# A graph-attention stack: when a one-head layer's row of G goes to memory and back

## The chip, the cores and the metric

The kernel runs on one core of a Trainium2 chip. The metric is the device time of one execution in microseconds (us). The core has five engines that run side by side: TensorE (PE in the profile, with its weight loads as PEld), VectorE (DVE), ScalarE (ACT), GpSimd (POOL) and SyncE (SP). SP issues nearly all DMA transfers of this kernel.

## The reference, cut to what matters

There are 16 graphs of 1024 nodes with 256 features, one adjacency matrix for all, and four layers. Each layer adds a graph-attention block to x:

```python
h = jnp.maximum(_layernorm(x), 0.0)
x = x + GNN(h, adj, W, a)
# in each GNN, with H heads (4, 1, 4, 1) of D = 256 / H features:
Wh = h @ W
e = leaky_relu(e_src[:, None] + e_dst[None, :])   # e_src, e_dst: Wh times the two halves of a
e = where(adj, e, -inf)
out = elu(softmax(e, axis=-1) @ Wh)               # relu in the last layer
```

Layers 0 and 2 have four heads, layers 1 and 3 have one. They differ in the slope of the leaky relu and in how adj becomes a mask.

## The kernel before, in words

**Softmax in factors.** exp(leaky_relu(s + d)) is a maximum of two products. The kernel therefore needs no exponential per pair of nodes. It has, for every node as a neighbour, a column factor `rcol` and a scale that is multiplied into `whx` (the projected features with a column of ones for the row sums), and for every node as a receiver a factor `gcol`. A tile of weights is `w = max(g, rcol) * mask`, where `g` is gcol laid out as a row and repeated on all 128 partitions. One DVE instruction makes 128 neighbours by 1024 receivers (`weights`, L455). TensorE then multiplies such tiles with `whx` and accumulates in PSUM (`aggregate`, L472), and ACT copies the sums out (L487).

**How G becomes a row.** `gcol` is spread over partitions. `rows` (L397 to L406) turns it on TensorE (L402), copies the result from PSUM to the tile `gT` on ACT (L404), and has SP write it to a buffer in device memory, `grow` (L406). `fetch` (L425 to L431) reads `grow` back repeated on all partitions, into `gs` (512 KB, L430). The fetch must wait until the write has landed. `broadcast` (L433 to L441) copies `gs` into the PSUM tile `g` on ACT (L441). For a four-head layer `gT` has 32 rows and there are four fetches; for a one-head layer it has 8 rows and there is one.

**How a layer's input is prepared.** `preparation(n)` lists 21 pieces: statistics of the two halves of x; normalise half 0 and half 1 (L334); then for each half a transposition, and eight projections of 128 nodes (`project`, L376 on TensorE, L378 on ACT); then `factors` (gcol, L394 and L395), `rows`, `fetch_heads`, and an empty piece. In nearly all layers the transposition is done by a DMA: `split` has ACT separate the 16-bit halves of the words (L343) and SP issue a transposing transfer (L345); `merge` has ACT put the halves together again (L351), which waits for that transfer. Each preparation has two such transfers, one a half.

**Order of the work.** Each graph is a stream of four layers; four streams are in flight and `order_of_steps` interleaves them, so that from step 7 on nearly all steps alternate between a four-head and a one-head layer of different graphs. A step is eight groups of matmuls. For a one-head layer a group is 128 receivers; for a four-head layer it is half the receivers of one head. Every engine gets its instructions in the order in which the program emits them, and works through them in that order; waits on semaphores do the rest.

Preparation runs ahead: step n is prepared while steps n - 2 and n - 1 aggregate. A table of due times, one number a piece, says behind which group each piece is emitted: `start = 8 * (n - 2)`, and `ONE`, `FOUR`, `NEXT`, `TIGHT` and others are the tables (L51 to L59). `ONE` is used by most one-head layers. Pieces fall due by time, and at the same time in the order of the steps (the sort at L611). A due time of 8 or more lies in the step just before, so 11 is behind group 3 of the four-head step n - 1.

Around the change, in a four-head step n - 1, the pieces of two layers meet: the end of the preparation of the one-head layer n (projections 4 to 7 and factors, behind group 0), and the start of the preparation of the four-head layer n + 1 (normalise and split of half 0 behind group 0, of half 1 behind group 1, merge of half 0 behind group 3, merge of half 1 behind group 4, its first four projections behind group 5). Fetches are limited by `fetch_heads`, which keeps at most two heads ahead of the G that has been copied, and `gs` has two buffers. PSUM has four banks for sums, projections and the transposed gcol, which are taken in turn (`bank`).

Of the kernel before, what the change touches and what calls it, by code (L numbers as in the profile page):

```python
# [50 lines left out]
FOUR = (-8, -8, -5, 0, 1, 0, 3, 5, 5, 5, 5, 1, 4, 5, 5, 5, 5, 6, 8, 8, 10)  # L51
SHORT = (-4, -4, -4, 0, 1, 0, 3, 5, 5, 5, 5, 1, 4, 5, 5, 5, 5, 6, 8, 8, 10)
NEXT = (-4, -4, -4, 1, 3, 2, 5, 8, 8, 8, 8, 4, 7, 8, 8, 8, 8, 9, 10, 10, 12)
ONE = (2, 2, 2, 3, 4, 3, 5, 7, 7, 7, 7, 4, 7, 8, 8, 8, 8, 8, 11, 11, 12)
SOON = (0, 0, 0, 1, 2, 1, 3, 4, 4, 5, 5, 2, 5, 6, 6, 7, 7, 7, 8, 8, 10)
FIRST = (-4, -4, -4, -2, -0.9, -1, -1, -0.8, -0.8, -0.8, -0.8, 0, 0, 1, 1, 1, 1, 1, 2, 2, 4)
TIGHT = (4, 4, 4, 5, 6, 5, 7, 8, 8, 8, 8, 6, 8, 9, 9, 9, 9, 9, 10, 10, 12)
# [13 lines left out]
def kernel(ctx: ExitStack, tc: tile.TileContext, x, adj, ws, avs, out):  # L71
# [417 lines left out]
    def slack(n):  # L489

        return LAYERS[steps[n + 1][1]][0] == 1
# [153 lines left out]
    for n, (b, l) in enumerate(steps):  # L645
# [6 lines left out]
        start = 8 * (n - 2)  # L652
        kind = ONE if LAYERS[l][0] == 1 else SOON if n < 3 else FOUR
        if kind is FOUR and free > start + kind[0]:
            kind = SHORT if slack(n - 2) else NEXT
        if kind is ONE and free > start + kind[0]:
            kind = TIGHT
# [120 lines left out]
```

## Time and profile before

| | us |
|---|---|
| median of 3 runs | 2448.24 |
| lowest, highest | 2442.77, 2450.0 |
| the profiled execution | 2449.74 |
| its span, first to last instruction | 2448.0 |

| engine | busy us | share of the span |
|---|---|---|
| PE (matmul) | 2394.8 | 98% |
| PEld (weight load) | 2153.2 | 88% |
| DVE | 2040.0 | 83% |
| ACT | 1480.0 | 60% |
| POOL | 1073.7 | 44% |

The granted clock of TensorE was 0.997 of full speed. All numbers of the profile are from one execution. Busy time is time in which an engine has an instruction under way; for TensorE, whose matmuls overlap, the gaps say more than the busy share. A wait is written as "engine, tile, line <- what released it", with the total, the count and the longest. The chain is found by going back from the last instruction to what released each. "SPq" is SP's queue of DMA instructions; a DMA's landing is a time of its own, later than its issue.

### The profile page before, as it was taken

To read this page: it belongs to the slowest core of one execution; us is meant where nothing else is said; L and a number is where in the kernel's file an instruction comes from. 1 tells how busy PE (TensorE), PEld (TensorE's weight loads), DVE (VectorE), ACT (ScalarE), POOL (GpSimd) and SP (SyncE) were. 2 spreads that over 40 slices of the span, in tenths; PEclk is the share of its full clock that TensorE was granted. 3 is DMA by queue.
4 is the path that set the end of the run, shared out by engine and by line. 5 is a ranking of instruction groups with operands and counts; after the bars stand their busy time and mean duration, and the time that the engine had idled before them with its cause. 6 is when DMAs were issued, how large, how long until landed. Compare 5 with 4: busy or idle time off the path is not lost.

```text
span 2448.0 us, 86681 instructions
## 1 busy us (share of the span) xinstructions
PE 2394.8 (98%) x39177; PEld 2153.2 (88%) x39177; DVE 2040.0 (83%) x2141; ACT 1480.0 (60%) x2505; POOL 1073.7 (44%) x1350
## 2 busy tenths in 40 slices
PE   7999999999999999999999999999999999999999
PEld 5888899899888888898998888888988998988987
DVE  8988588898888988887988888888889888888794
ACT  5465676565666656765656765566655577656542
POOL 3345455433345454544433554543443345545331
PEclk9999999999999999999999999999999999999999
DMA  5322233243333222323433322224334323223220
GB/s 182 83 53 63 45 79 67 66 114 92 85 96 79 72 63 52 74 71 96 114 89 88 80 62 71 64 50 108 75 93 114 95 48 80 68 65 76 75 54 35
DMA packets 292220, 191.84 MB, mean 78 GB/s; under 512 B 261778, under 2 KB 264586, under 8 KB 289930
## 3 DMA queue, kind: packets, MB, share of 16 engines
q1 hardware_dynamic: 291840, 186.29, 30.6%
q8 instruction: 307, 5.03, 0.9%
q14 instruction: 63, 0.52, 0.1%
q10 hardware_dynamic: 10, 0.00, 0.0%
HBM read 104.87 MB, written 17.43 MB: 50 GB/s over the span
## 4 chain that ended last, share of the span: by engine, by line
PE 82%; ACT 7%; DMA 5%; DVE 4%; issue 2%; POOL 0%; SPq 0%; DVEq 0%; ACTq 0%
PE bank L472 64%; PE bank L376 17%; DVE w L455 2%; DMA gs<-grow 2%; ACT rows L334 2%; DMA grow<-gT 2%; ACT g L441 1%; ACT rows L343 1%; ACT rows L525 1%; ACT rows L351 1%; ACT y L487 1%; DVE bn L287 1%; DMA rows<-rows 0%; PE bank L402 0%; ACT whx L378 0%
## 5 line engine op out<-in xcount | busy, mean ns | idle before, releaser
L472 PE MATMUL bank<-whx,w 128*64 128x65 f32 x36864 | 1898.0, 240 | 17.9 <-DVE w L455 9.3
L472 PEld LDWEIGHTS bank<-whx,w 128*64 128x64 f32 x36864 | 1745.7, 144 | 173.9 <-ACT whx L378 21.8
L455 DVE SCALAR_TENSOR_TENSOR w<-g,rcol,mask 128x1024 f32<-128x1024 f32 (+1 forms) x1288 | 1540.2, 1270 | 204.0 <-PE bank L472 165.2
L388 POOL TENSOR_TENSOR whx<-whx 128x1024 f32<-128x1024 f32 x128 | 244.5, 1910 | 819.1 <-ACT whx L386 819.1
L487 ACT ACTIVATE y<-bank 128x260 f32<-128x260 f32 (+1 forms) x504 | 192.1, 381 | 567.7 <-PE bank L472 567.7
L376 PE MATMUL bank<-wx,rows 128*128 128x264 f32 (+1 forms) x2048 | 484.8, 390 | 15.4 <-ACT y L487 11.8
L376 PEld LDWEIGHTS bank<-wx,rows 128*128 128x128 f32 x2048 | 380.9, 190 | 90.9 <-ACT y L487 17.9
L519 POOL TENSOR_TENSOR y<-y,r 128x1024 f32<-128x1024 f32 x124 | 259.0, 2098 | 222.0 <-DVE rows L518 188.4
L334 ACT ACTIVATE rows<-x,shift,rstd 128x256 f32<-128x256 f32 x512 | 265.2, 591 | 66.7 <-POOL shift L328 62.2
L378 ACT ACTIVATE whx<-bank 128x264 f32<-128x264 f32 (+1 forms) x512 | 193.7, 388 | 184.9 <-PE bank L376 184.6
L532 POOL TENSOR_TENSOR x<-x,rows 128x1024 f32<-128x1024 f32 x94 | 222.4, 2365 | 177.9 <-DVE rows L531 177.9
L351 ACT ACTIVATE rows<-rows 128x2048 uint16<-128x2048 uint16 x122 | 261.6, 2144 | 22.7 <-DMA rows<-rows 22.6
L343 ACT ACTIVATE rows<-rows 128x2048 uint16<-128x2048 uint16 x122 | 233.3, 1912 | 3.9
L531 DVE SCALAR_TENSOR_TENSOR rows<-rows,y 128x1024 f32<-128x1024 f32 x94 | 186.6, 1986 | 42.8 <-ACT rows L525 39.1
L287 DVE BATCH_NORM_STATS2 bn<-x 128x6 f32<-128x256 f32 x512 | 175.8, 412 | 34.5 <-POOL x L532 31.1
L441 ACT ACTIVATE g<-gs 128x1024 f32<-128x1024 f32 x158 | 161.8, 1024 | 67.1 <-DMA gs<-grow 55.9
L322 POOL TENSOR_TENSOR rstd<-rstd,neghalf 128x4 f32<-128x4 f32 (+1 forms) x97 | 121.3, 1251 | 41.1 <-DVE shift L323 33.8
L525 ACT ACTIVATE rows<-rows 128x1024 f32<-128x1024 f32 x96 | 100.7, 1048 | 4.2 <-DVE rows L554 4.2
L508 DVE RECIPROCAL r<-y 128x32 f32<-128x32 f32 (+1 forms) x63 | 17.4, 277 | 100.9 <-ACT y L487 100.9
L518 DVE SCALAR_TENSOR_TENSOR rows<-y,r 128x1024 f32<-128x1024 f32 x58 | 70.2, 1251 | 1.1
L386 ACT ACTIVATE whx<-whx,nbias 128x16 f32<-128x16 f32 (+1 forms) x128 | 40.4, 316 | 4.2
L384 ACT ACTIVATE rcol<-whx,rbias 128x16 f32<-128x16 f32 (+1 forms) x128 | 40.0, 313 | 4.2
(82 smaller groups left out, 461.9 us busy)
## 6 DMA issues: line engine op xcount, KB each, us to landing
gs<-grow SPq DMA_DIRECT2D x158, 512.0 KB
x<-in_x SPq DMA_DIRECT2D x15, 1024.0 KB
out<-x SPq DMA_DIRECT2D x30, 512.0 KB
w<-in_adj SPq DMA_DIRECT2D x8, 512.0 KB
rows<-rows SPq DMA_TRANSPOSE x122
x<-in_x SPq DMA_DIRECT2D x2, 512.0 KB
wx<-in_L_gnn_W SPq DMA_DIRECT2D x8, 128.0 KB
out<-x SPq DMA_DIRECT2D x8, 128.0 KB
```

The source lines that it names most:

```text
L287: nc.vector.bn_stats(bn[:, c, :], xs[b][:, c, :])
L334: nc.scalar.activation(xn[:, :, q, :], xs[b][:, c, :].rearrange("p (k i) -> p k i", k=K), AF.Relu, bias=st["shift"][:, c:c + 1], scale=st[ ...
L343: nc.scalar.activation(bits, xn.rearrange("p (n s) -> p s n", s=2), AF.Copy)
L351: nc.scalar.activation(st["hT", half].rearrange("p k i -> p (k i)").bitcast(U16).rearrange("p (n s) -> p n s", s=2), st["turned", half].re ...
L376: nc.tensor.matmul(pw, lhsT=st["hT", half][:, k, q * P:(q + 1) * P], rhs=wx[l][:, k, :], start=(k == 0), stop=(k == K - 1))
L378: nc.scalar.activation(st["whx"][:, c, :], pw, AF.Copy)
L388: nc.gpsimd.tensor_tensor(wh[:, :, :, 0:D], wh[:, :, :, 0:D], wh[:, :, :, D:D + 1].to_broadcast([P, HALF, H, D]), op=ALU.mult)
L455: nc.vector.scalar_tensor_tensor(state[n]["w", h, j][:, s], state[n]["g", h][:, s], state[n]["rcol"][:, j, h:h + 1], masks[LAYERS[steps[n] ...
L472: nc.tensor.matmul(acc[o % P:o % P + cols, q, :], lhsT=st["w", h, jc][:, o:o + cols], rhs=st["whx"][:, jc, h * (D + 1):(h + 1) * (D + 1)], ...
L487: nc.scalar.activation(st["y"][:, i0:i0 + per, h, :], acc, AF.Copy)
L519: nc.gpsimd.tensor_tensor(yh, yh, rb, op=ALU.mult)
L532: nc.gpsimd.tensor_add(xh, xh, e)
```

## The change

One table of due times is edited. In `ONE`, the pieces `rows` and `fetch_heads` (the 19th and 20th numbers) are due at 9 in place of 11. Pieces of the same due time are emitted in the order of the steps, so both come ahead of the normalise and split of half 1 of layer n + 1, which are due at the same time.

```diff
-ONE = (2, 2, 2, 3, 4, 3, 5, 7, 7, 7, 7, 4, 7, 8, 8, 8, 8, 8, 11, 11, 12)
+ONE = (2, 2, 2, 3, 4, 3, 5, 7, 7, 7, 7, 4, 7, 8, 8, 8, 8, 8, 9, 9, 12)
```

## The prediction

> **What bounds the kernel now.** I read the page first (busy shares, then the chain that ended last), next the waits by pair of engines, then the chain and the ACT timeline inside one period.
>
> ```profile
> PE 2394.8 (98%) x39177; PEld 2153.2 (88%) x39177; DVE 2040.0 (83%) x2141; ACT 1480.0 (60%) x2505; POOL 1073.7 (44%) x1350
> ...
> PE 82%; ACT 7%; DMA 5%; DVE 4%; issue 2%; POOL 0%; SPq 0%; DVEq 0%; ACTq 0%
> ```
>
> TensorE sets the time: it is idle for 2448.0 - 2394.8 = 53.2 us, and in the trace some 30 us of that lie in the start and the tail. From 400 to 2330 us its gaps over 0.1 us add up to only 17.8 us. So whatever the change does to DMAs or ACT, it can gain no more than TensorE gaps that it removes. The waits say which those are:
>
> ```profile
> ACT g L441 <- DMA gs<-grow: 55.9, 29, 4.6
> ...
> DVE w L455 <- ACT g L441: 24.5, 14, 11.9
> ...
> PE bank L376 <- ACT y L487: 11.8, 14, 2.0
> ```
>
> The columns are the total in us, the count and the longest. ACT waits 29 times for the fetched row of G (gs); TensorE waits 14 times, 11.8 us in all, at a projection (L376) for ACT's L487. One period of a four-head and a one-head layer shows that these are one thing. Its chain (start, us, what):
>
> ```profile
> 1544.70 1.05 ACT rows L525
> 1545.76 0.27 ACT y L487
> 1546.03 0.15 ACT gT L404
> 1546.17 0.36 SPq L345
> 1546.54 0.05 issue
> 1546.59 3.33 DMA grow<-gT
> 1549.92 0.02 issue
> 1549.94 4.59 DMA gs<-grow
> 1554.53 0.02 issue
> 1554.56 1.03 ACT g L441
> 1555.58 0.31 ACT y L487
> 1555.89 0.04 issue
> 1555.94 4.72 PE bank L376 x20
> ```
>
> and ACT in the same stretch:
>
> ```profile
> 1540.52 2.07 ACT L334 ACTIVATE rows<-x,shift,rstd 128x256 f32<-128x256 f32 x4
> 1542.61 1.91 ACT L343 ACTIVATE rows<-rows 128x2048 uint16<-128x2048 uint16 x1
> ...
> 1549.85 2.16 ACT L351 ACTIVATE rows<-rows 128x2048 uint16<-128x2048 uint16 x1 [0.80 <-DMA rows<-rows]
> 1554.56 1.03 ACT L441 ACTIVATE g<-gs 128x1024 f32<-128x1024 f32 x1 [2.54 <-DMA gs<-grow]
> ```
>
> ACT works in order: second merge (L351, waits for the second transposing transfer), copy of G (L441, waits for gs), then the L487 that frees the PSUM bank which the fourth projection needs. TensorE did three projections (12 matmuls) and then stood 0.44 us, from 1555.50 to 1555.94. Two transfers therefore end ahead of that L487, the fetch of gs and the second transpose, and gs now ends last by 2.54 us.
>
> **What the skill says.** The Trainium skill, DMA: Bandwidth & Descriptors, section "Queues, rings and completion order": SP owns one row of rings, and each DMA engine takes a ring's descriptors in ring order. The trace agrees: the grow write, issued 2.04 us behind the second transpose, landed 0.15 us after it (1549.92 against 1549.77, from the completion events). The same page, "Two DMAs through the same engine are not ordered": a DMA that reads what another wrote needs its completion semaphore. So SP must stand at the gs issue until grow has landed; here it did, from 1547.4 to 1549.94. And "Rules for kernel authors": a transpose beside ordinary DMAs needs no extra care, so nothing but ring order and that SP wait keeps the two apart.
>
> **The change, part by part.** No instruction is added or removed. The built order has four moves in 28 of 31 one-head layers. TensorE's 8-row transpose (L402) goes from behind group 3 to behind group 1 of the four-head layer; ACT's gT copy (L404) goes ahead of the second normalise (L334 x4); SP's grow write and gs fetch go ahead of the second transpose. DVE and POOL are unchanged.
>
> - *TensorE's transpose*: 0.27 us either way. Its operand gcol is ready (ACT L395 ends 1534.53, group 1 ends near 1537) and its bank was freed by a projection's copy. Without that lead it would stand about 1 us a layer; the trace has 2 us of it. Cost 0.
> - *ACT*: the copy starts at 1540.52, 5.4 us sooner than 1545.92. It delays the second normalise and split by 0.15 us (L404 at 1545.92, its follower at 1546.07).
> - *SP and the grow write*: issued at 1540.8, behind the first transpose (issued 1538.47, landed 1544.39). By ring order it lands at 1544.39 + 0.17 = 1544.56. SP issues gs at 1544.6.
> - *The wait added*: the second transpose now queues on SP behind the gs issue, which waits for grow. Its data are ready at 1544.67 (L343's end plus 0.15); SP is free at 1544.6 + 0.4 = 1545.0. It goes out at 1545.0 in place of 1544.55. Over 27 periods worked out alike, this delay is 0.2 us in 15 and at most 1.8. Behind it on SP stand stores and a load of x in some periods, else nothing for over 20 us.
> - *The rings*: gs's 4 KB packets run from 0.6 to about 3.0 us after its issue (1550.5 to 1553 in this period); a transpose's packets begin 1.17 us after its own. The trace of before has no transpose just behind a gs fetch in the steady part, so I bound it. Low end: they share engines freely, 0. High end: the transpose starts when gs's packets end, 1544.6 + 3.0 - (1545.0 + 1.17) = 1.4 us later. One case at the start, a transpose issued 1.67 us after a gs, began 2.6 us after issue instead of 1.17 and landed 7.35 us after it; that speaks for the high end, which I take.
> - *Then ACT*: the second transpose took 5.22 us from issue to landing here (4.2 to 6.3 over the periods, median 5.5). It lands at 1545.0 + 5.22 + 1.4 = 1551.6, where it landed at 1549.77. Merge to 1553.7, G copy without a wait to 1554.7 (gs landed near 1549), L487 ends at 1555.05, 0.84 us sooner than 1555.89. TensorE wanted the bank at 1555.50: the 0.44 us go, with 0.45 to spare.
>
> The same sum for each of the 27 periods from 330 to 2330 us: before, TensorE stands 10.9 us in all (11.8 with the smaller waits that the view counts there); after, 1.3 us, in three periods. With the low end of the rings it is 0. L487 is 3.1 us sooner at best (near 1108) and 1.7 us later at worst (near 581, where TensorE had 1.8 us in hand). So the sum is -9.7 us at the high end of the rings and -10.9 at the low. Landings of the second transpose scatter by 2 us from period to period and will fall differently; I take 1.2 us off for that: **-8.5 us**. On the profiled execution (2449.74 us, span 2448.0) that is 2441.2; on the median of the runs, 2448.24, which is 1.5 us less, 2439.7. I say 2440. The stall that goes leaves TensorE's own work as the next limit; nothing is late behind it, since DVE has its G sooner too.
>
> **Rivals.**
>
> - *The second transpose takes gs's place.* For it: it is the other transfer ahead of the same L487, it is delayed by SP's wait and by gs's packets, and in 14 of the 27 periods TensorE had no gap to give back. Against: gs ends up to 4.6 us behind it now. If it lands 1.2 us later than I worked out in every period, the waits become 11.4 us in place of 10.9: no gain, 2449. At half of that, about -6. This case: 2442 to 2451.
> - *Slower.* The same place, past its break-even of 1.2 us: merge L351 late, L487 late, and TensorE stands at the fourth projection in nearly every period, also where it does not now. At 1.5 us later than worked out the sum is +6.1 us (2454); at 2.0 us it is +19 (2467). The price rises steeply since all 27 periods then pay. It needs a transpose to be slowed by more than ring order: the case at the start of the kernel landed 7.35 us after its issue, and 6.5 is the mean that I already have.
> - *The change doesn't do what it says*: the gs buffer or the limit on fetches ahead could hold the fetch back. The built order has the fetch straight behind the write, and its buffer's last reader, ACT's copy for head 2, ended near 1523. Excluded; what remains would be within 0.3%.
>
> **How the numbers follow.** Case one, -7 to -11 us (2437 to 2441.5): 0.44. The transpose eats the gain: 0.35. Slower: 0.21. A measurement of this kernel tells about 0.3% (7.3 us) from no change, so faster means below 2440.9 and slower above 2455.6. Most of case one is faster (0.40), its rest and case two are the same (0.41), and of case three 0.19 passes the bound. The range runs from 2435 (all 11.8 us gone, and runs as low as before's lowest against its median, leaving out 0.05) to 2457, which leaves out the worse part of the slow case, about 0.13. The likeliest case alone: 2436 to 2443.
>
> **What would show it.** Right: ACT's wait for gs at L441 (55.9 us) falls to a third or less; TensorE's wait at L376 for L487 falls from 11.8 to 1 to 3 us; ACT's wait at the second L351 for its transpose grows from under 1 to about 2 us a period; the grow write lands just after the first transpose. Wrong: a wait at L376 of 10 us or more with ACT's L351 behind a transpose (first rival), TensorE gaps at L376 in over 20 periods (second), or DMA time of the transposes from issue to landing over 8 us. A loss with no more waiting at L376 would mean something that I have not seen: gaps in TensorE's own instruction supply ("issue", 6.7 us at L472 now) while gs and transposes crowd the DMA engines.

## The result, and the profile after

The changed kernel is slower. Its median is 2457.06 us (12 runs, 2454.53 to 2465.24) against 2444.06 us for the kernel before on the same chips (12 runs, 2436.89 to 2454.72). The ratio is 1.0053, 95% interval 1.0036 to 1.0069. The forecast was 2440, in a range of 2435 to 2457.

The profiled execution of the changed kernel took 2462.47 us, with a span of 2460.7, which is 12.7 us more than before. Both profiled executions lie some 5.5 us over the median of their twelve runs, so the two profiles can be held against each other. These are the lines of its page that answer to those of before, busy shares and chain:

```profile
PE 2397.4 (97%) x39177; PEld 2159.4 (88%) x39177; DVE 2039.2 (83%) x2141; ACT 1480.1 (60%) x2505; POOL 1073.3 (44%) x1350
...
PE 92%; DVE 4%; issue 2%; ACT 1%; DMA 0%; DVEq 0%; ACTq 0%
```

The DMAs are gone from the chain that ended last (5% before, 0% now) and ACT is nearly gone (7% before). TensorE is nearly all that is left (92%), and still the kernel is longer. Two waits of the kernel before, to compare with (total us, count, longest):

```profile
ACT rows L351 <- DMA rows<-rows: 22.6, 22, 2.2
...
PE bank L472 <- issue: 6.7, 12, 1.8
```

The waits of the changed kernel:

```profile
ACT rows L351 <- DMA rows<-rows: 61.3, 26, 4.4
PEld bank L472 <- issue: 46.7, 67, 2.4
PE bank L472 <- issue: 31.0, 28, 2.3
...
ACT g L441 <- DMA gs<-grow: 3.1, 3, 1.6
...
PE bank L376 <- ACT y L487: 0.7, 1, 0.7
```

Three of these lines went the way that was forecast. ACT's wait for gs fell from 55.9 us to 3.1, TensorE's wait at the projections from 11.8 to 0.7, and ACT's wait for the transposes grew from 22.6 to 61.3. The new line is TensorE's wait for "issue", that is, for nothing that the profile shows: 6.7 us before, 31.0 now.

The account closes. These are the two groups of TensorE on the page, before and then after (busy us, mean ns, idle time ahead, what ended most of it):

```profile
L472 PE MATMUL bank<-whx,w 128*64 128x65 f32 x36864 | 1898.0, 240 | 17.9 <-DVE w L455 9.3
...
L376 PE MATMUL bank<-wx,rows 128*128 128x264 f32 (+1 forms) x2048 | 484.8, 390 | 15.4 <-ACT y L487 11.8
```

```profile
L472 PE MATMUL bank<-whx,w 128*64 128x65 f32 x36864 | 1901.7, 241 | 41.3 <-issue 31.0
...
L376 PE MATMUL bank<-wx,rows 128*128 128x264 f32 (+1 forms) x2048 | 483.3, 391 | 2.0 <-ACT rows L366 0.8
```

By these groups, the idle time ahead of the aggregating matmuls (L472) went from 17.9 to 41.3 us, that ahead of the projections (L376) from 15.4 to 2.0, and TensorE's busy time from 2394.8 to 2397.4. That is +23.4 - 13.4 + 2.6 = +12.6 us, of the span's 12.7.

One period shows what TensorE waits for. First TensorE, then SP's DMA issues (start, us):

```profile
1542.81 11.02 PE L472 MATMUL bank<-whx,w 128*64 128x65 f32 x372
1555.64 3.60 PE L472 MATMUL bank<-whx,w 128*64 128x65 f32 x116 [1.82 <-issue]
```

```profile
1543.60 1.76 SPq L345 DMA_TRANSPOSE rows<-rows  x1
1545.91 0.53 SPq L406 DMA_DIRECT2D grow<-gT  x1
1549.50 0.35 SPq L430 DMA_DIRECT2D gs<-grow  x1
1549.96 4.82 SPq L345 DMA_TRANSPOSE rows<-rows  x1
```

The DMA packets in the trace hold a second queue beside SP's, with 16 KB packets. The page names it (packets, MB, share of the engines' time):

```profile
q8 instruction: 307, 5.03, 0.9%
```

Its bytes fit TensorE's instructions: 5.03 MB over its 2 x 39,177 matmuls and weight loads is 64 bytes each, so a packet is a block of 256 instructions. The same period worked out from the packets, with the time in which most of each transfer's packets ran:

```
1543.60  first transpose issued    packets 1544.77 to 1547.23
         block of instructions             1547.43 to 1548.31
1549.50  gs issued                 packets 1550.50 to 1552.86
1549.96  second transpose issued   packets 1552.17 to 1556.29
         block of instructions             1553.25 to 1554.19
         TensorE stands                    1553.83 to 1555.64
         block of instructions             1557.11 to 1558.04
```

A four-head layer uses up a block of 128 matmuls and 128 weight loads in some 3.8 us (384 such matmuls take 11.37 us in the chain of the kernel before, 29.6 ns each). Here two blocks are 5.8 us apart: from 1550.50 until the late block starts, packets of gs and of the second transpose run without a pause, and TensorE runs dry for 1.82 us. That the burst is the reason is tested below. It goes on 1.45 us after the late block is in. In the 28 gaps of over 0.1 us at L472 between 300 and 2340 us, that time from the end of a block to TensorE's next matmul is always between 1.22 and 1.59 us. In the kernel before, the blocks of the corresponding period started at 1546.47 (just after the second transpose began), 1549.91 (its end) and 1553.68 (the end of gs), 3.4 and 3.8 us apart.

One more reading shows that these waits are waits for blocks. Here TensorE stood three times in a row (in brackets, the wait ahead of each line):

```profile
1850.71 3.95 PE L472 MATMUL bank<-whx,w 128*64 128x65 f32 x127 [0.25 <-issue]
1855.65 3.95 PE L472 MATMUL bank<-whx,w 128*64 128x65 f32 x128 [0.99 <-issue]
1860.77 0.57 PE L472 MATMUL bank<-whx,w 128*64 128x65 f32 x12 [1.16 <-issue]
```

The numbers of recorded TensorE instructions ahead of the three are 59,841, 60,097 and 60,353: 256 apart, one block each. The same holds for all 28 waits for issue at L472 in this trace: from one to any other it is a whole multiple of 256 instructions. So it is for the 12 of the kernel before, whereas its 14 waits for ACT's L487 at L376 are spread over the block.

### The profile page after: what moved, and what is told of

Same layout as the page of the kernel before. It is cut to its first block, busy times and chain, and to the rows that moved or that the text cites. A ratio compares the mean times of both kernels' runs of the same rounds, so it can differ in the third digit from the quotient of the medians.

```text
span 2460.7 us, 86666 instructions
## 1 busy us (share of the span) xinstructions
PE 2397.4 (97%) x39177; PEld 2159.4 (88%) x39177; DVE 2039.2 (83%) x2141; ACT 1480.1 (60%) x2505; POOL 1073.3 (44%) x1350
## 3 DMA queue, kind: packets, MB, share of 16 engines
q8 instruction: 307, 5.03, 0.9%
## 4 chain that ended last, share of the span: by engine, by line
PE 92%; DVE 4%; issue 2%; ACT 1%; DMA 0%; DVEq 0%; ACTq 0%
PE bank L472 72%; PE bank L376 19%; DVE w L455 3%; DVE bn L287 1%; ACT rows L334 0%; PE bank L402 0%; ACT rows L351 0%; DMA rows<-rows 0%; DVE mask L260 0%; DVE rows L531 0%; DMA x<-in_x 0%; ACT mask L264 0%; DVE rows L554 0%; ACT rows L343 0%; PE bank L210 0%
## 5 line engine op out<-in xcount | busy, mean ns | idle before, releaser
L472 PE MATMUL bank<-whx,w 128*64 128x65 f32 x36864 | 1901.7, 241 | 41.3 <-issue 31.0
L472 PEld LDWEIGHTS bank<-whx,w 128*64 128x64 f32 x36864 | 1748.8, 144 | 198.3 <-issue 46.7
L487 ACT ACTIVATE y<-bank 128x260 f32<-128x260 f32 (+1 forms) x504 | 191.9, 381 | 575.9 <-PE bank L472 575.9
L376 PE MATMUL bank<-wx,rows 128*128 128x264 f32 (+1 forms) x2048 | 483.3, 391 | 2.0 <-ACT rows L366 0.8
L376 PEld LDWEIGHTS bank<-wx,rows 128*128 128x128 f32 x2048 | 383.4, 191 | 72.7 <-ACT rows L351 7.2
L351 ACT ACTIVATE rows<-rows 128x2048 uint16<-128x2048 uint16 x122 | 262.0, 2147 | 63.0 <-DMA rows<-rows 61.3
```

What stands on the lines that cost most here:

```text
L351: nc.scalar.activation(st["hT", half].rearrange("p k i -> p (k i)").bitcast(U16).rearrange("p (n s) -> p n s", s=2), st["turned", half].re ...
L376: nc.tensor.matmul(pw, lhsT=st["hT", half][:, k, q * P:(q + 1) * P], rhs=wx[l][:, k, :], start=(k == 0), stop=(k == K - 1))
L472: nc.tensor.matmul(acc[o % P:o % P + cols, q, :], lhsT=st["w", h, jc][:, o:o + cols], rhs=st["whx"][:, jc, h * (D + 1):(h + 1) * (D + 1)], ...
L487: nc.scalar.activation(st["y"][:, i0:i0 + per, h, :], acc, AF.Copy)
```

## The experiments

Theory A says that TensorE starves for instructions. Theory B says that the order itself is the harm: SP's wait makes the second transpose late, and the merge and the projections behind it with it. Every ratio is to the kernel before, with its 95% interval; waits are from one profile each.

**The burst made short.**

```diff
-        gs = state[n]["gs", h] = work.tile([P, N], F32, name="gs", bufs=2)
-        nc.sync.dma_start(out=gs, in_=state[n]["grow"][h].rearrange("c i -> (c i)")
-                          .partition_broadcast(P))
+        gs, m = work.tile([P, N], F32, name="gs", bufs=2), P if LAYERS[steps[n][1]][0] == 1 else N
+        nc.sync.dma_start(out=gs[:, 0:m], in_=state[n]["grow"][h].rearrange("c i -> (c i)")[0:m]
+                          .partition_broadcast(P)); state[n]["gs", h] = gs[:, 0:m]
...
-        nc.scalar.activation(g, state[n]["gs", h], AF.Copy)
+        nc.scalar.activation(g.rearrange("p (c i) -> p c i", c=C), state[n]["gs", h][:, None, :].to_broadcast([P, C, P]) if LAYERS[steps[n][1]][0] == 1 else state[n]["gs", h].rearrange("p (c i) -> p c i", c=C), AF.Copy)
```

> The changed kernel, but a one-head layer fetches 128 of its 1024 columns of G (64 KB in place of 512 KB), and ACT repeats them when it copies G; so G of the one-head layers is not the right one, and every other instruction stays. Theory A (TensorE starves for instructions: a 16 KB block of them cannot be fetched while gs and the second transpose fill the DMA engines back to back): TensorE's wait at L472 for issue falls from 31.0 us to 10 or less, its wait at L376 stays at 2 or less, the time is 18 to 26 us under the changed kernel, ratio to before about 0.996. Theory B (the order itself: SP's wait and the later second transpose delay the merge): TensorE's gaps stay at 25 us or more and the ratio at 1.004 to 1.006.

A second run takes 4 * P columns in place of P, repeated twice:

> The changed kernel with half of a one-head layer's row fetched (512 of 1024 columns, 256 KB), which ACT repeats; so G of the one-head layers is not the right one. Theory A: TensorE's wait for issue at L472 lies between that of 64 KB (9.7 us) and that of 512 KB (31.0 us), 14 to 24 us; ratio to before 0.998 to 1.003. If a threshold decides and not the length of the burst, it is like one of the two ends.

With 64 KB the ratio is 0.9969 (0.9956 to 0.9981), with 256 KB 0.9995 (0.9984 to 1.0006), with all 512 KB it is the change's 1.0053. ACT's wait for the transposes and TensorE's wait in each profile, 64 KB first:

```profile
ACT rows L351 <- DMA rows<-rows: 36.1, 27, 2.8
...
PE bank L472 <- issue: 9.7, 17, 1.3
```

```profile
ACT rows L351 <- DMA rows<-rows: 46.2, 28, 3.5
...
PE bank L472 <- issue: 14.3, 17, 1.5
```

The wait grows with the bytes: 9.7, 14.3, 31.0. The order of instructions, SP's wait for grow and all counts are the change's in each. With the burst short, the changed order is about what the prediction said it would be, some 7 us faster; no run has the short burst in the order of before, so how much of the 7 us comes from the fewer bytes is not known. Theory B expected TensorE's gaps to stay. These two runs alone do not rule it out, because with fewer bytes the second transpose is less late too (ACT's waits above, against 61.3 us). The run with a pause, below, parts the two.

**The burst made without the change.** A write of the split half to spare memory goes out ahead of the second transpose, in the four-head layers or in the one-head layers:

```diff
             st["turned", half] = prep.tile([P, 2, K * HALF, P], U16, name="rows", bufs=HBUFS)
+            if half == 1 and H > 1 and n > 8:      # the second run: H == 1
+                nc.sync.dma_start(out=dram.tile([P, 2, K * HALF * P], U16, name="spare"), in_=bits)
             nc.sync.dma_start_transpose(
```

> The kernel before, with one more transfer and nothing else: 512 KB from SBUF to a spare buffer in device memory, issued just ahead of the second transpose of each four-head layer from step 9 on, so that the DMA engines have two full transfers back to back with G's path as before. Theory A: TensorE's wait at L472 for issue rises from 6.7 to 25 to 40 us. The second transpose, the grow write and gs all come some 2 us later as well, so its wait at L376 rises from 11.8 to 30 to 60 us; time +40 to +80 us, ratio 1.016 to 1.033. Theory B: the wait at L376 rises alike, the wait for issue stays under 10.

> The same additional 512 KB, but ahead of the second transpose of each one-head layer, which runs while TensorE works on a one-head step and needs a block of instructions only every 25 us or so (128 matmuls at 217 ns). Theory A: the wait at L472 for issue stays under 10 us and the time within 0.3% of before (ratio 0.997 to 1.003). If it is DMA traffic as such that costs, the ratio is like that of the same bytes in the four-head step.

In the four-head layers' transposes the ratio is 1.0125 (1.0106 to 1.0143). This is its profile:

```profile
PE bank L472 <- issue: 20.8, 24, 1.8
PE bank L376 <- ACT y L487: 18.1, 18, 2.0
```

In the one-head layers' it is 0.9991 (0.9981 to 1.0001), with this wait:

```profile
PE bank L472 <- issue: 5.7, 11, 1.4
```

The same bytes cost over 30 us of median time in one place and nothing that can be measured in the other. The sizes in the first were overestimated (20.8 against 25 to 40, 18.1 against 30 to 60, and the ratio under its 1.016 to 1.033), the direction of both was right. Not all of its cost is starving: its profile is 24.1 us longer than that of before (span 2472.1), the wait for issue is 14.1 us longer and the wait at L376 6.3; there the transfer also stands ahead of grow and gs. What else differs between the two places is how fast TensorE uses up instructions while the transfers run: 29.6 ns a matmul in a four-head layer, 217 ns in a one-head layer (112 of them take 24.33 us in the chain of the kernel before).

**A pause put between the two.** The bytes and the order of the change, but SP must wait until gs has landed before it issues the second transpose:

```diff
-ONE = (2, 2, 2, 3, 4, 3, 5, 7, 7, 7, 7, 4, 7, 8, 8, 8, 8, 8, 11, 11, 12)
+ONE = (2, 2, 2, 3, 4, 3, 5, 7, 7, 7, 7, 4, 7, 8, 8, 8, 8, 8, 9, 9, 12)
...
+            if half == 1 and H > 1 and n > 8 and LAYERS[steps[n - 1][1]][0] == 1 and ("gs", 0) in state[n - 1]:
+                nc.sync.dma_start(out=dram.tile([1, P], F32, name="mark"), in_=state[n - 1]["gs", 0][0:1, 0:P])
             nc.sync.dma_start_transpose(
```

> The changed kernel with a pause between the two transfers, and no fewer bytes: SP sends 512 bytes of gs to a spare buffer in device memory ahead of the second transpose, from step 9 on, so that SP waits until gs has landed and the second transpose goes out some 3.4 us later than in the changed kernel. Theory A: between the two a block of instructions gets through, TensorE's wait for issue at L472 falls from 31.0 to 12 us or less, although everything behind the transpose is later than ever: ACT's wait at L351 grows from 61 to over 100 us and TensorE's waits at L376 from under 2 to 10 to 40 us; ratio 1.000 to 1.010. Theory B (the late second transpose is the harm): it is the worst of all, with the gaps where the changed kernel has them, at L472, and 50 us or more there; ratio over 1.012.

The ratio is 1.0102 (1.0085 to 1.0119), just past the upper edge that was expected for A and under what was expected for B. The waits decide:

```profile
ACT rows L351 <- DMA rows<-rows: 107.8, 28, 6.2
...
PE bank L376 <- ACT y L487: 28.5, 21, 3.4
...
PE bank L472 <- issue: 3.8, 8, 0.9
```

The starving is gone (31.0 to 3.8) with not a byte less, and the cost of a late transpose stands at L376 (0.7 to 28.5), not at L472 as theory B expected. In the changed kernel the second transpose was late too, but not late enough to reach TensorE. The two mechanisms are thus both real, each leaves its own line, and the changed kernel pays for the starving.

**Half of the change, and half of its step.**

```diff
-ONE = (2, 2, 2, 3, 4, 3, 5, 7, 7, 7, 7, 4, 7, 8, 8, 8, 8, 8, 11, 11, 12)
+ONE = (2, 2, 2, 3, 4, 3, 5, 7, 7, 7, 7, 4, 7, 8, 8, 8, 8, 8, 9, 11, 12)    # r9f11
+ONE = (2, 2, 2, 3, 4, 3, 5, 7, 7, 7, 7, 4, 7, 8, 8, 8, 8, 8, 10, 10, 12)   # r10
```

> Half of the change: the row is turned, copied and written two groups sooner, the fetch stays due at 11, so SP has grow, second transpose, gs. The fetch no longer waits for grow and goes out about 2 us behind the second transpose's issue, so its packets follow the transpose's without a pause. Theory A: the wait at L472 for issue rises to 15 to 30 us, the wait at L376 falls from 11.8 to 5 or less, ratio 1.000 to 1.006. Theory B (only what is ahead of the transpose hurts): the transpose is not delayed, the wait for issue stays under 10 and the ratio is 0.995 to 0.998.

> The change at half its step: both pieces due at 10, behind group 2, so that on SP they stay behind the second transpose and only the copy on ACT is sooner. Theory A: the transfers stay apart, the grow write lands behind the second transpose as before, gs at most 1 us sooner: wait at L376 8 to 12 us, wait for issue 6 to 10, ratio 0.998 to 1.001. If being two groups sooner was the harm and not being ahead of the transpose, half the loss is seen: 1.002 to 1.003.

With the early write alone the ratio is 1.0004 (0.9994 to 1.0014), the wait for issue 11.8 us and the wait at L376 for L487 1.3 us. The ratio and the wait at L376 are as theory A had them; the wait for issue lies between the two forecasts (15 to 30, under 10): gs behind the transpose starves TensorE less than gs ahead of it. In the period looked at, a block got in as the transpose began (1538.79) and the next as gs ended (1544.38), 5.6 us apart. With both pieces at 10 the ratio is 1.0007 (0.9995 to 1.0019), the wait for issue 6.6 and at L376 8.7, as theory A had it. Being one group sooner, with the order on SP as before, does no harm.

**What was sought, without the burst.** ACT copies group 5 out before it waits for gs:

```diff
-                upto = min(done["tiles"] + (6 if per > 1 else 3), done["free"] + WBUFS)
+                upto = min(done["tiles"] + (6 if per > 1 else 3), done["free"] + WBUFS,
+                           place[n, h, C - 1] + 9 if per > 1 and k == 4 else len(tiles))
```

> The kernel before, with all DMAs as they were, but the first weight tiles of a one-head layer (and with them ACT's copy of its G, L441) are emitted one group later, so that ACT copies out group 5 (L487) before it waits for gs. The PSUM bank that the fourth projection needs is then free in time, and the fifth's is the next to wait for ACT. What was sought from the change, without its burst: TensorE's wait at L376 for L487 falls from 11.8 us to about 4, its wait for issue at L472 stays at 6 to 9, DVE waits for G no longer than before; -5 to -8 us, ratio 0.997 to 0.998. If the wait for gs only moves on to the next projections or to DVE's tiles, the ratio is 0.999 to 1.002.

> Both: ACT's copy of G behind group 5, and the row turned and written two groups sooner with the fetch due at 11 as before. If the two remove the same wait at L376 (12 us in all), there is no more to gain than from one of them, and the wait for issue of the early write (11.8 us) stays: ratio 0.998 to 1.001. If the early write alone had lost its gain to something else, the sum is better than each: 0.995.

The first gives 0.9987 (0.9976 to 0.9998), a median of 2438.96 us; of the kernels that compute everything it is the only one that is faster than the kernel before by more than the noise, just so, and by less than expected. Its profile:

```profile
ACT g L441 <- DMA gs<-grow: 22.1, 21, 2.7
...
PE bank L472 <- issue: 6.6, 12, 1.2
...
PE bank L376 <- ACT y L487: 0.7, 1, 0.7
```

No DMA was moved, and the wait at L376 is as low as in the changed kernel. The two together give 1.0022 (1.0014 to 1.0029), slower than either and outside both forecasts. The early write brings its wait for issue (12.6 us), and there is nothing left for it to gain; but TensorE's busy time is also 4.7 us longer than with the early write alone (2396.7 against 2392.0), and the granted clock does not explain it (see the end). This stays open.

## Why the prediction was wrong

- **The four moves and their effect on ACT**: right. ACT's wait for gs fell to 3.1 us (forecast: a third of 55.9 or less), TensorE's wait at L376 to 0.7 (forecast 1 to 3).
- **SP's added wait, and the second transpose behind gs**: right, and near in size. In the period above gs was issued 5.9 us after the first transpose (forecast 6.1), the second transpose 0.46 us behind it (forecast 0.4), and its packets began 2.2 us after its issue in place of 1.17 (forecast 1.4 us later). One reading was off: gs's packets begin some 1.0 us after its issue, not 0.6 (1550.92 in the period of before, not 1550.5). ACT waited 3.0 us for the second transpose; over the kernel 61.3 us. That did not reach TensorE, so the first two rivals, which both ended at L376, did not occur.
- **The step that failed** is the term of the rings, which charged the burst of gs and the second transpose to the second transpose alone, and with it the sentence that nothing but ring order and SP's wait keeps the two apart (the row of the page that it follows is about wrong data, not about time). A third user of the same DMA engines was left out: TensorE's own instructions. Measured, that term is +24.3 us of waiting for issue. The last sentence of the prediction named such a gap as something not seen yet; it was on the page of before as the 16 KB queue and as 6.7 us of waiting, and was given no price.
- **The gain** was probably mis-sized too. The 11.8 us at L376 are one execution's, and that execution (2449.74 us) was 5.7 us over the median of the twelve runs (2444.06). Two kernels with nearly the order of before showed less at L376: 6.6 us with the write in the one-head layers (span 2438.5), 8.7 with both pieces at 10 (span 2441.0). The changed order with the short burst gained 6.8 us in the median (2435.93 against 2442.77), not far from the 8.5 of the sum. With one profile of the kernel before, this is likely and not shown.
- **The slow rival** had the right sign and the wrong mechanism and place. The range ended at 2457 and the median fell just beyond it, at 2457.06. That it came so near is luck: the range reached that far for a late transpose, whose waits at L376 did not occur.

The Trainium skill bears on this in a page that the prediction did not use, Runtime: NRT & Kernel Launch, section "Instruction fetch mechanics": an engine's instructions come in 16 KiB blocks by a DMA queue of its own, and this is said to be mostly hidden. The block size agrees with the 16 KB packets. That it is hidden does not hold here: 31.0 us of waiting, where 128 matmuls take 3.8 us. By DMA: Bandwidth & Descriptors, "Queues, rings and completion order", a DMA engine turns between its queues after each packet; in the periods shown above, a block started near the beginning or the end of a transfer. Elsewhere in the trace of before blocks also start in the middle of one (at 949.18, in a transpose whose packets ran from 947.43 to 951.25), so the traces do not speak against the page. How the burst holds a block back, by the engines' turns or by device memory, which gs and the blocks both might load, no run here shows.

## What to carry to other kernels

Where TensorE runs small matmuls, its instruction blocks are a stream with a deadline on the DMA engines: price any transfer that is moved by the pause that it closes, not only by its own landing. An "issue" wait on TensorE together with a full DMA record is read by the times of the 16 KB packets, and by whether the instruction counts at the gaps differ by multiples of 256. And a gain that is read from one execution's waits should be held against how far that execution lies from the median.

## What the runs showed of the hardware

- A matmul stream at 29.6 ns each needs a 16 KB block every 3.8 us or so, and TensorE goes on 1.2 to 1.6 us after a late block is in.
- The waits for issue at L472 stand at block borders: 28 of 28 in the changed kernel, 12 of 12 in the kernel before.
- Short gaps may also cost clock. In the changed kernel the granted clock was half for 3.4 us at 357.0 and at 1183.0 us, within 1.2 us of the ends of gaps of 2.07 and 2.10 us; that is, by an estimate from these figures, about 3.4 us of lost time, more than the 2.6 us by which TensorE's busy time grew. The early write alone had one such stretch, after a gap of 2.60 us; so had the last kernel of the experiments above, after 2.92 us, which accounts for none of the difference between them. In all eleven traces, between 300 and 2400 us, the half-clock stretches are seven, and each begins within 1.5 us of the end of a TensorE gap of 1.99 to 3.45 us. A gap of 2.26 us in the changed kernel had none, so length alone does not decide, and that the gap is the cause is not shown.
